# Pre-norm image blocks in four mixers: gate rows of the mLSTM cut into units, its second pass begun inside the first, and the norm of the neighbourhood layer one step ahead

## The chip, the cores and the metric

The kernel runs on one core of a Trainium2 chip, in 32-bit floats. The metric is device time in microseconds (us), the median of three runs. The engines are TensorE (PE), VectorE (DVE), ScalarE (ACT), GpSimd (POOL) and SyncE (SP). Each takes its instructions strictly in order, so an instruction that waits holds all behind it. Each also has a queue from which transfers (DMAs) are issued; here SP and ACT issue them.

## The reference

The input is a batch of 8 images of 32 x 32 tokens with 256 channels. Four layers follow, each `x = x + layer(groupnorm(x))`: retention, mLSTM, neighbourhood attention (7 x 7) and attention on a disc. The change touches the second and the third. The mLSTM, for each image with 1024 tokens, 8 heads and 512 inner channels, is cut to:

```python
up = xs @ W_up.T;  x_m, z = up[..., :512], up[..., 512:]
x_act = silu(conv_b + causal_conv4(x_m))
q, k, v = blockwise 4x4 projections of x_act, x_act, x_m
ig, fg = [q, k, v] @ W_i.T + b_i, [q, k, v] @ W_f.T + b_f
lc = cumsum(log_sigmoid(fg))
logD = where(causal, lc[i] - lc[j] + ig[j], -inf);  m = max_j logD
C = (q k^T / sqrt(64)) * exp(logD - m)
h = (C / (max(|sum_j C|, exp(-m)) + eps)) v
out = ((layernorm(h) * norm_w + skip * x_act) * silu(z)) @ W_down.T
```

The neighbourhood layer adds a learned bias for each head and relative position to the scores of a token with its 49 neighbours and takes a softmax over them.

## The kernel before

Each layer is a function (`layer0` to `layer3`). Activations are kept with channels on the 128 partitions. Between the layers they lie in DRAM, one image as a tile of 128 x 2 x 1024. A ring of three such tiles (`Base.big`, L170) holds images and the large weights in turn: a new tile of the ring waits until the tile three back has been read for the last time.

**mLSTM, `layer1` (L734).** The order of PE and ACT is the order of the program. The order of DVE, POOL and SP is set by a planner from its own costs, so an instruction may stand earlier or later on these than it does in the program. The work runs over 16 segments, each half an image (512 tokens), in two passes.

The first pass is a loop over units `u`, a quarter of a segment each: `project` (PE L808, ACT copy xm L823), `convolve` (ACT L830, three DVE instructions L835), `silu_a` two units later (ACT L841), `silu_z` (L848). In each segment `gates(s-1)` (PE L859, DVE copy L865, four stores from SP L869) makes the gate values of the segment before. Beside it run the group norm of the next image (DVE L194, PE L203, DVE L211, PE L222, POOL L226 and L239) and its load.

The gates of four images make 32 rows of 1024 tokens, one for each head of each image. `rows_sum` (L882) fetches them (SP L892), takes the logarithm of the sigmoid (ACT L895 to L898, DVE), a running sum (DVE L899), a running maximum (L903), stores the maximum and makes three differences (L910 among them). `rows_exp` (L913) takes the exponentials (ACT L917), stores two of them, and turns two row tiles so that tokens lie on partitions (PE L926, DVE L929). For the first four images they are called after `u` = 40 and 46; for the last four in the second pass, before the chunks 1 and 3.

The second pass is a loop over 64 chunks of 128 tokens, four a segment. `load(s)` fetches the activations xa (SP L983), rows of exponentials (low and rb, L993) and xm (xv, L999); `maxima(n)` fetches a 128 x 1024 tile d (L1010), from which POOL makes the masked difference (L1013) and ACT eight exponentials (L1022). In a chunk PE takes `scores` (L1080), whose product with d is DVE's L1086; `queries` of the next chunk (PE L1035, ACT copy g L1037, DVE gr L1040); `keys` (PE L1048, DVE L1052); `value` (PE L1062, ACT copy L1066); then `within` (L1099, L1105), which needs d, `across` (L1119, L1125), which needs gr, and `update` (L1150, POOL L1165, DVE L1169). `units` puts output work of the segment before between them: one part in the chunks t = 0, 1 and 3 of four, none in t = 2; t = 3 has `down` (L1205). PSUM results of one bank's size share a ring of four buffers. `follow(k)` prepares the next layer's first image, k chunks before the end: load at k = 7, statistics (L194) at 5, later the norm and weights.

**Neighbourhood layer, `layer2` (L1619).** It works in 16 steps an image. Here PE, ACT, DVE and POOL are all in program order. Its first instructions are loads from the ACT queue: parameters (L1636), a mask table `win` (L1638), the bias for eight heads (L1641) and the projection's weights (L1643). The bias used is `win - bias` on POOL (L1774), as scores are kept with the opposite sign; the mask table excludes tokens that are no neighbours. Then PE projects (L1667) and ACT or DVE copies with a bias (L1673, L1681, L1683). In a step n the order is: scores of n+1 (PE L1407, DVE L1416), the exponentials of n (ACT L1428) and their division (POOL L1433, `e`), then the `Fillers` units that are due (a unit with due step `at` is emitted in the first step n for which `at <= n`), then the transposes of n-1 (L1447) and the values of n-2 (L1466). Projections of image b start at step 16b - 8; the two halves of its norm (`normed`, POOL L239) are due at 16b - 9 and 16b - 8.5.

Of the kernel before, what the change touches and what calls it, by code (L numbers as in the profile page):

```python
# [16 lines left out]
P = 128  # L17
# [15 lines left out]
def shape_constants():  # L33
# [44 lines left out]
    idx = near_index()  # L78
    k["k_win2"] = np.where(idx >= 0, 0.0, -MASK_OUT).astype(f)


# [28 lines left out]
def layouts(inputs):  # L110
# [29 lines left out]
    a["l2_rpb"] = np.where(idx[:, None] >= 0, rpb[:, idx].transpose(1, 0, 2), 0.0).astype(  # L140
# [593 lines left out]
def layer1(tc, K, src, dst, n_img, a, first):  # L734
# [3 lines left out]
    with tc.tile_pool(name="l1c", bufs=1, reuse_waits="tile") as cp, tc.tile_pool(  # L738
        name="l1w", bufs=1, reuse_waits="tile"
    ) as wk, tc.tile_pool(  # L740
# [11 lines left out]
        def load_x(b):  # L752
            x[b] = K.big("x")
            nc.scalar.dma_start(x[b], src[:, :, b * L : (b + 1) * L])
# [127 lines left out]
        def rows_sum(i):  # L882
            def temps(tag):
                t = wk.tile([P, 2, L], F32, tag=tag, name="row", bufs=2)
                return t[0:NR, 0], t[0:NR, 1]

            (av, f), (sp, lc) = temps("num"), temps("sq")
            cm = wk.tile([NR, 1 + L], F32, name="cm")
            row[i] = av, f, sp, lc, cm
            for g, t in enumerate((av, f)):  # L890
                for b in range(GRP):
                    nc.sync.dma_start(t[8 * b : 8 * b + 8], gated[i][b, g])  # L892
            nc.vector.memset(cm[:, 0:1], MASK_OUT)
            nc.scalar.preload_act_table_set("natural_log_exp_and_others")
            nc.scalar.activation(sp, f, AF.Abs, bias=gbias[0:NR, 1:2])  # L895
            nc.vector.tensor_scalar(f, f, gbias[0:NR, 1:2], 0.0, ALU.add, ALU.min)
            nc.scalar.activation(sp, sp, AF.Exp, scale=-1.0)
            nc.scalar.activation(sp, sp, AF.Ln, bias=epsn[0:NR, 1:2])  # L898
            nc.vector.tensor_tensor_scan(lc, f, sp, 0.0, ALU.add, ALU.subtract)  # L899
            nc.vector.scalar_tensor_tensor(  # L900
                av, av, gbias[0:NR, 0:1], lc, ALU.add, ALU.subtract
            )
            nc.vector.tensor_tensor_scan(cm[:, 1:], av, av, cm[:, 0:1], ALU.max, ALU.max)  # L903
            nc.sync.dma_start(rowd[i][0], cm[:, 1:])


            ends = by_chunk(cm[:, 1:])[:, :, P - 1 : P].to_broadcast([NR, 2 * NCH, P])
            starts = by_chunk(cm[:, 0:L])[:, :, 0:1].to_broadcast([NR, 2 * NCH, P])
            nc.vector.tensor_sub(by_chunk(sp), starts, by_chunk(cm[:, 1:]))
            nc.vector.tensor_sub(by_chunk(f), by_chunk(av), ends)  # L910
            nc.vector.scalar_tensor_tensor(lc, lc, -1.0, cm[:, 1:], ALU.mult, ALU.subtract)

        def rows_exp(i):  # L913
            av, w, r, low, _ = row.pop(i)
            nc.scalar.preload_act_table_set("natural_log_exp_and_others")
            for t in (r, w, low):
                nc.scalar.activation(t, t, AF.Exp)  # L917
            nc.sync.dma_start(rowd[i][1], r)
            nc.sync.dma_start(rowd[i][2], low)

            ps = ring("col_ps")[:, 0 : 2 * 2 * NCH * NR].rearrange(
                "p (i t n) -> p i t n", i=2, n=NR
            )
            for j, t in enumerate((av, w)):
                for k in range(2 * NCH):
                    nc.tensor.transpose(  # L926
                        ps[:, j, k], t[:, k * P : (k + 1) * P], K.ident[0:NR, 0:NR]
                    )
# [1284 lines left out]
```

## Time and profile before

| | us |
|---|---|
| median of three runs | 3490.29 (3487.11 to 3499.76) |
| the profiled execution | 3481.33 |
| its span, first to last instruction | 3479.5 |
| PE busy | 3255.0 |
| ACT busy | 2237.1 |
| DVE busy | 2172.7 |
| POOL busy | 1491.2 |
| mean granted PE clock | 0.964 |
| layer 0 ends, mLSTM's first pass starts | about 1088 |
| second pass starts | about 1373 |
| layer 2 starts | about 2039 |

The clock is a share of full speed. A group in the page names line, engine, operation, output and inputs, shape and count, then busy time and mean, then the idle time of the engine ahead of it with what ended that. A line of the timeline gives start, duration, engine, line, operation, shape and the number of instructions drawn together; in brackets stands the idle time ahead of it and the instruction that ended it.

### The profile page before, as it was taken

The numbers are of one execution on the slowest core, as the hardware profiler recorded it, in microseconds if no ns is written. First come the engines' busy times: TensorE is split into PE (matmuls) and PEld (weight loads), VectorE is DVE, ScalarE is ACT, GpSimd is POOL, SyncE is SP. The second block draws the span as 40 slices with busy tenths as digits, with TensorE's granted clock in tenths as the row PEclk, the third lists the DMA queues.
The fourth block names the chain that finished last, engine by engine and source line by source line (L and its number), as shares of the span: only waits on it lengthen the run. The fifth ranks groups of instructions, "written<-read, shape, count | busy, mean of one in ns | idle before, by whom it ended". The sixth has DMA issues, their size and how long they took to land.

```text
span 3479.5 us, 77392 instructions
## 1 busy us (share of the span) xinstructions
PE 3255.0 (94%) x30760; PEld 1655.6 (48%) x30760; DVE 2172.7 (62%) x5559; ACT 2237.1 (64%) x5022; POOL 1491.2 (43%) x1071
## 2 busy tenths in 40 slices
PE   7999999999998988899999989999998889999998
PEld 3323323323323444677676645555553545555454
DVE  4777677677675664555555545556564667677775
ACT  3667667667675554555555446666675778888885
POOL 4233233232221110345444443333335567777777
PEclk9999999999999998899999999999998889999999
DMA  3000000000003667577777531111111001101001
GB/s 135 13 25 1 25 25 1 25 25 1 25 25 116 236 199 256 162 199 179 203 210 187 136 112 38 38 38 50 50 48 43 2 14 38 32 29 35 26 26 59
DMA packets 139054, 268.44 MB, mean 77 GB/s; under 512 B 9218, under 2 KB 77188, under 8 KB 130372
## 3 DMA queue, kind: packets, MB, share of 16 engines
q1 hardware_dynamic: 131152, 241.90, 23.1%
q10 hardware_dynamic: 7540, 21.60, 1.9%
q8 instruction: 242, 3.96, 0.5%
q14 instruction: 120, 0.98, 0.1%
HBM read 178.27 MB, written 85.20 MB: 76 GB/s over the span
## 4 chain that ended last, share of the span: by engine, by line
PE 68%; ACT 10%; DVE 8%; DMA 5%; POOL 4%; issue 4%; SPq 0%; POOLq 0%; ACTq 0%; DVEq 0%
PE s L633 7%; PE sm L651 6%; PE num L678 5%; PE qkv_ps L1667 5%; PE qkv_ps L1902 4%; PE up_ps L808 3%; PE dn_ps L1205 3%; PE qk_ps L508 3%; DMA x<-x 3%; PE pt L1575 2%; PE pt L1447 2%; PE fac_ps L2004 2%; PE o_ps L561 2%; ACT e L1963 2%; DMA d<-l1rows 2%
## 5 line engine op out<-in xcount | busy, mean ns | idle before, releaser
L639 DVE TENSOR_TENSOR e<-s,ret 128x1024 f32<-128x1024 f32 x512 | 603.0, 1219 | 180.3 <-PE s L633 175.1
L643 ACT ACTIVATE ea<-e 128x1024 f32<-128x1024 f32 x512 | 535.9, 1056 | 267.0 <-DVE e L639 233.4
L633 PE MATMUL s<-qk,qk 32*128 32x512 f32 x2048 | 300.2, 640 | 2.6 <-POOL qk L525 1.9
L1580 DVE COPY pts<-pt 112x512 f32<-112x512 f32 x256 | 176.5, 690 | 181.0 <-PE pt L1575 179.1
L1433 POOL TENSOR_TENSOR e<-e,su 128x616 f32<-128x616 f32 (+2 forms) x128 | 157.4, 1230 | 287.0 <-DVE su L1432 278.8
L1013 POOL TENSOR_TENSOR d<-cmask,d 128x1024 f32<-128x1024 f32 x64 | 152.7, 2386 | 296.0 <-DMA d<-l1rows 183.5
L651 PE MATMUL sm<-ea,ones 128*32 128x512 f32 x2048 | 273.0, 604 | 2.0 <-DVE dn L659 2.0
L678 PE MATMUL num<-e,v 128*32 128x512 f32 x2048 | 266.6, 592 | 0.0
L808 PE MATMUL up_ps<-x,wup 128*128 128x512 f32 x512 | 233.5, 608 | 11.3 <-DVE gate L865 9.3
L1963 ACT ACTIVATE e<-win,disc 128x196 f32<-128x196 f32 x512 | 240.9, 548 | 0.2
L1565 POOL TENSOR_TENSOR e<-e,su 128x784 f32<-128x784 f32 x128 | 191.5, 1496 | 92.3 <-DVE su L1564 67.4
L1557 ACT ACTIVATE e<-e,mx 128x196 f32<-128x196 f32 x512 | 229.1, 456 | 0.0
L1970 POOL TENSOR_TENSOR e<-e,win 128x784 f32<-128x784 f32 x128 | 201.3, 1573 | 38.1 <-issue 32.9
L1667 PE MATMUL qkv_ps<-x,w 128*128 128x512 f32 x384 | 194.7, 644 | 21.3 <-POOL x L239 17.5
L1428 ACT ACTIVATE e<-e,mx 128x154 f32<-128x154 f32 (+2 forms) x512 | 213.4, 429 | 0.2 <-DVE mx L1416 0.2
L1902 PE MATMUL qkv_ps<-xq,w 128*128 128x512 f32 x384 | 199.5, 646 | 11.0 <-DVE kp L1914 5.4
L1575 PEld LDWEIGHTS pt<-idg,e 128*112 128x112 f32 x1024 | 121.1, 141 | 136.9 <-issue 60.1
L1575 PE MATMUL pt<-idg,e 128*112 128x128 f32 x1024 | 167.3, 290 | 19.2 <-DVE pts L1580 8.8
L633 PEld LDWEIGHTS s<-qk,qk 32*128 32x128 f32 x2048 | 85.1, 182 | 184.2 <-issue 121.5
L835 DVE SCALAR_TENSOR_TENSOR cv<-xm,par,cv 128x512 f32<-128x512 f32 x192 | 140.2, 750 | 48.8 <-ACT cv L830 46.2
L1022 ACT ACTIVATE d<-d,cols 128x128 f32<-128x128 f32 x512 | 164.1, 395 | 0.0
L1547 DVE CUSTOM_DVE_ANT_0 e<-s,e 128x196 f32<-128x196 f32 x512 | 154.0, 358 | 12.9 <-PE s L1534 7.8
(241 smaller groups left out, 6644.1 us busy)
## 6 DMA issues: line engine op xcount, KB each, us to landing
d<-l1rows SPq DMA_DIRECT2D x64, 512.0 KB
x<-x SPq DMA_DIRECT2D x25, 1024.0 KB
x<-x SPq DMA_DIRECT2D x32, 512.0 KB
l1xm<-xm SPq DMA_DIRECT2D x16, 1024.0 KB
l1sz<-sz SPq DMA_DIRECT2D x16, 1024.0 KB
xv<-l1xm SPq DMA_DIRECT2D x32, 512.0 KB
l1xa<-xa SPq DMA_DIRECT2D x16, 1024.0 KB
sz<-l1sz SPq DMA_DIRECT2D x16, 1024.0 KB
```

What stands on the lines that cost most here:

```text
L633: nc.tensor.matmul(s[:, j % 2], qk[b, 1, c][g, kb * P : (kb + 1) * P], qk[b, 0, c][g, h * HALF : (h + 1) * HALF], start=True, stop=True,)
L639: nc.vector.tensor_mul(e[n, i], s, m)
L643: nc.scalar.activation(ea[n, i], e[n, i], AF.Abs)
L651: nc.tensor.matmul(acc["sm"][g, :], ones, ea[n, j // 2][:, j % 2, :], start=kb == 0, stop=kb == 7,)
L678: nc.tensor.matmul(acc["num"][g, :], v[b][:, kb, vc], e[n, j // 2][:, j % 2, :], start=kb == 0, stop=kb == 7,)
L808: nc.tensor.matmul(ps, wup[:, kc, m * P : (m + 1) * P], seg(s)[:, kc], start=kc == 0, stop=kc == 1,)
L1428: self.nc.scalar.activation(p[:, j], p[:, j], AF.Exp, scale=-1.0, bias=mx[:, j : j + 1], accum_out=su[:, j : j + 1],)
L1557: self.nc.scalar.activation(e[:, j], e[:, j], AF.Exp, scale=-1.0, bias=mx[:, j : j + 1], accum_out=self.su[:, j : j + 1],)
L1575: self.nc.tensor.transpose(ps[: self.PART, at : at + P], self.tile(n)[:, 2 * i + j, k * self.PART : (k + 1) * self.PART], self.K.ident,)
L1667: nc.tensor.matmul(ps, w[:, kc, o : o + P], x[b][:, kc, h * HALF : (h + 1) * HALF], start=kc == 0, stop=kc == 1,)
L1902: nc.tensor.matmul(ps, w[:, kc, o : o + P], xq[b][:, kc, h * HALF : (h + 1) * HALF], start=kc == 0, stop=kc == 1,)
L1963: nc.scalar.activation(e[:, j], win[:, 0], AF.Tanh, scale=disc[b][:, i, 8 + h : 9 + h], bias=disc[b][:, i, h : h + 1],)
```

## The change

- mLSTM: the memory of the working tiles is laid out ahead of the constants', and the second image has a tile of its own instead of one of the ring.
- `rows(i)` replaces `rows_sum` and `rows_exp`: eleven units with the same instructions. For the first four images one is called in each `u` from 36 to 46. For the last four they follow the chunks 0, 1, 2, 2, 3, 3, 4, 4, 5, 6 and 7, in tiles of the ring.
- `start()`, at `u` = 58 of 67, issues the second pass's first load, three d tiles and two masked differences; queries, keys and values of chunk 0 are taken at `u` = 66, ahead of the last `gates`. The load of rb is a function of its own, `load_rb`, so that segment 0's stays behind the last gates.
- In the second pass the image for the residual is loaded at the first chunk of its image, four chunks later than before. `value(n+1)` follows `within(n)`. The next layer's image is loaded at k = 12 for k = 7.
- Layer 2: the bias table holds the mask value itself, the table `win` is gone, and only the sign is turned, for heads 0 and 1 on ACT, for the others on POOL. `normed` is due half a step earlier, which puts its second half in step 16b - 9 with the first.

The diff, cut; `load`, `load_z`, `maxima`, `masked`, `decays`, `queries`, `keys` and `value` move up unchanged, but for `load`, which loses the rb part and the image:

```diff
@@ -137,7 +133,7 @@
     a["l2_par"] = np.concatenate([_cols(qkv_b), _cols(i["L2_conv_proj_b"])], 1)
     idx = near_index()
     rpb = i["L2_conv_rpb"].reshape(HEADS, -1)
-    a["l2_rpb"] = np.where(idx[:, None] >= 0, rpb[:, idx].transpose(1, 0, 2), 0.0).astype(
+    a["l2_rpb"] = np.where(idx[:, None] >= 0, rpb[:, idx].transpose(1, 0, 2), MASK_OUT).astype(
         rpb.dtype
     )
     a["l3_qkv"] = _wt(i["L3_conv_w_qkv"])
@@ -735,9 +731,9 @@
     nc = tc.nc
     NS = 2 * n_img
     GRP = min(4, n_img)
-    with tc.tile_pool(name="l1c", bufs=1, reuse_waits="tile") as cp, tc.tile_pool(
-        name="l1w", bufs=1, reuse_waits="tile"
-    ) as wk, tc.tile_pool(
+    with tc.tile_pool(name="l1w", bufs=1, reuse_waits="tile") as wk, tc.tile_pool(
+        name="l1c", bufs=1, reuse_waits="tile"
+    ) as cp, tc.tile_pool(
         name="l1p", bufs=1, space=PSUM, reuse_waits="tile"
     ) as pp, tc.manual_schedule(
         engines={mybir.EngineType.PE, mybir.EngineType.Activation}
@@ -749,8 +745,8 @@
         K.ring = ring
         x, xm, xa, sz, conv = ({} for _ in range(5))
 
-        def load_x(b):
-            x[b] = K.big("x")
+        def load_x(b, own=False):
+            x[b] = wk.tile([P, 2, L], F32, name="x1") if own else K.big("x")
             nc.scalar.dma_start(x[b], src[:, :, b * L : (b + 1) * L])
 
         def seg(s):
@@ -879,58 +875,211 @@
         def by_chunk(t):
             return t.rearrange("p (t n) -> p t n", n=P)
 
-        def rows_sum(i):
...
+        def rows(i, temp):
+            q = {}
+            def fetch():
+                for k in ("av", "f"), ("sp", "lc"):
+                    t = temp()
+                    q[k[0]], q[k[1]] = t[0:NR, 0], t[0:NR, 1]
+                q["cm"] = wk.tile([NR, 1 + L], F32, name="cm")
+                for g, k in enumerate(("av", "f")):
+                    for b in range(GRP):
+                        nc.sync.dma_start(q[k][8 * b : 8 * b + 8], gated[i][b, g])
+                nc.vector.memset(q["cm"][:, 0:1], MASK_OUT)
+            def soft():
+                f = q["f"]
+                nc.scalar.activation(q["sp"], f, AF.Abs, bias=gbias[0:NR, 1:2])
+                nc.vector.tensor_scalar(f, f, gbias[0:NR, 1:2], 0.0, ALU.add, ALU.min)
+            def soft2():
+                sp = q["sp"]
+                nc.scalar.preload_act_table_set("natural_log_exp_and_others")
+                nc.scalar.activation(sp, sp, AF.Exp, scale=-1.0)
+                nc.scalar.activation(sp, sp, AF.Ln, bias=epsn[0:NR, 1:2])
+            def sums():
+                nc.vector.tensor_tensor_scan(
+                    q["lc"], q["f"], q["sp"], 0.0, ALU.add, ALU.subtract
+                )
+            def a():
+                nc.vector.scalar_tensor_tensor(
+                    q["av"], q["av"], gbias[0:NR, 0:1], q["lc"], ALU.add, ALU.subtract
+                )
+            def most():
+                av, cm = q["av"], q["cm"]
+                nc.vector.tensor_tensor_scan(cm[:, 1:], av, av, cm[:, 0:1], ALU.max, ALU.max)
+                nc.sync.dma_start(rowd[i][0], cm[:, 1:])
+            def before():
+                cm = q["cm"]
+                starts = by_chunk(cm[:, 0:L])[:, :, 0:1].to_broadcast([NR, 2 * NCH, P])
+                nc.vector.tensor_sub(by_chunk(q["sp"]), starts, by_chunk(cm[:, 1:]))
+            def within():
+                ends = by_chunk(q["cm"][:, 1:])[:, :, P - 1 : P]
+                nc.vector.tensor_sub(
+                    by_chunk(q["f"]), by_chunk(q["av"]), ends.to_broadcast([NR, 2 * NCH, P])
+                )
+            def low():
+                nc.vector.scalar_tensor_tensor(
+                    q["lc"], q["lc"], -1.0, q["cm"][:, 1:], ALU.mult, ALU.subtract
+                )
+            def exps():
+                nc.scalar.preload_act_table_set("natural_log_exp_and_others")
+                for k in ("sp", "f", "lc"):
+                    nc.scalar.activation(q[k], q[k], AF.Exp)
+                nc.sync.dma_start(rowd[i][1], q["sp"])
+                nc.sync.dma_start(rowd[i][2], q["lc"])
+            def turned():
+                ps = ring("col_ps")[:, 0 : 2 * 2 * NCH * NR].rearrange(
+                    "p (i t n) -> p i t n", i=2, n=NR
+                )
+                for j, k in enumerate(("av", "f")):
+                    for t in range(2 * NCH):
+                        nc.tensor.transpose(
+                            ps[:, j, t], q[k][:, t * P : (t + 1) * P], K.ident[0:NR, 0:NR]
+                        )
+                nc.vector.tensor_copy(cols[i], ps)
+            return [fetch, soft, soft2, sums, a, most, before, within, low, exps, turned]
...
+        def load_rb(s):
+            b, h = divmod(s, 2)
+            rows, r8 = rowd[b // GRP], 8 * (b % GRP)
+            rb[s] = wk.tile([P, 4, 3 + HALF], F32, tag="xm", name="rb", bufs=2)
+            for p in range(2):
+                r = rows[1][r8 + p : r8 + p + 1, h * HALF : (h + 1) * HALF]
+                nc.sync.dma_start(
+                    rb[s][64 * p : 64 * p + 64, :, 0:HALF],
+                    bass.AP(r.tensor, r.offset, [[0, 64], [2 * L, 4], [1, HALF]]),
+                )
...
+        def start():
+            load_x(0)
+            load(0)
+            for n in range(3):
+                maxima(n)
+            masked(0)
+            masked(1)
         with tc.tile_pool(name="l1g", bufs=1, space=PSUM, reuse_waits="tile") as gp:
             if n_img > 1:
-                load_x(1)
+                load_x(1, True)
+            units = {}
+            for i in range(NG - 1):
+                todo = rows(i, lambda: wk.tile([P, 2, L], F32, tag="num", name="row", bufs=2))
+                for k, f in enumerate(todo):
+                    units.setdefault(8 * GRP * (i + 1) + 4 + k, []).append(f)
             for u in range(4 * NS + 3):
                 s, c = divmod(u, 4)
                 if s < NS:
@@ -949,124 +1098,28 @@
                     silu_a(*divmod(u - 2, 4))
                 if u < 4 * NS:
                     silu_z(s, c)
+                if NG > 1 and u == 4 * NS - 6:
+                    start()
+                if NG > 1 and u == 4 * NS + 2:
+                    queries(0)
+                    keys(0)
+                    value(0)
                 if c == 2 and s:
                     gates(s - 1)
-                i, k = divmod(u - 8 * GRP, 8 * GRP)
-                if 0 <= i < NG - 1 and k == 8:
-                    rows_sum(i)
-                if 0 <= i < NG - 1 and k == 14:
-                    rows_exp(i)
+                for f in units.get(u, []):
+                    f()
         nc.scalar.preload_act_table_set("natural_log_exp_and_others")
+        late = rows(NG - 1, lambda: K.big("row"))
         if NG == 1:
-            rows_sum(0)
-            rows_exp(0)
...
+            for f in late:
+                f()
+            start()
+            queries(0)
+            keys(0)
+            value(0)
+            late = []
+        at = (0, 1, 2, 2, 3, 3, 4, 4, 5, 6, 7)
+        late = {n: [f for m, f in zip(at, late) if m == n] for n in range(2 * NCH)}
...
@@ -1227,7 +1280,7 @@
             def follow(k):
 
                 nx = K.next
-                if k == 7:
+                if k == 12:
                     nx.load()
                 if k == 5:
                     for i in range(4):
@@ -1243,26 +1296,18 @@
 
             def prefetch(n):
                 s, t = divmod(n, NCH)
+                if n and n % (2 * NCH) == 0:
+                    load_x(s // 2)
                 if t == 0 and s + 1 < NS:
                     load(s + 1)
+                    load_rb(s + 1)
                 if t == 3 and s < NS:
                     load_z(s)
 
-            load(0)
-            for n in range(3):
-                maxima(n)
-            masked(0)
-            masked(1)
-            queries(0)
-            keys(0)
-            value(0)
+            load_rb(0)
             decays(0, range(4))
             for n in range(N):
                 prefetch(n)
-                if NG > 1 and n == 1:
-                    rows_sum(NG - 1)
-                if NG > 1 and n == 3:
-                    rows_exp(NG - 1)
                 if n + 3 < N:
                     maxima(n + 3)
                 if n + 2 < N:
@@ -1274,14 +1319,16 @@
                 if n + 1 < N:
                     decays(n + 1, (0, 1))
                     keys(n + 1)
-                    value(n + 1)
                 units(n, 1)
                 within(n)
                 if n + 1 < N:
+                    value(n + 1)
                     decays(n + 1, (2, 3))
                 units(n, 2)
                 across(n)
                 update(n)
+                for f in late.get(n, []):
+                    f()
                 if K.next:
                     follow(N - n)
             for n in range(N, N + NCH):
@@ -1634,8 +1681,6 @@
         x[0], w = first.x, first.w
         par = cp.tile([P, 8], F32, name="par2")
         nc.scalar.dma_start(par, a["l2_par"])
-        win = cp.tile([P, nbias], F32, name="win2")
-        nc.scalar.dma_start(win, a["k_win2"])
         bias = cp.tile([P, HEADS, nbias], F32, name="bias2")
         for h in range(HEADS):
             nc.scalar.dma_start(bias[:, h], a["l2_rpb"][:, h])
@@ -1697,6 +1742,12 @@
                     t[:, 704:].rearrange("p (s i j) -> p s i j", s=2, j=14), cols(5, 8, 14)
                 )
 
+        def negated(h):
+            if h < 2:
+                nc.scalar.activation(bias[:, h], bias[:, h], AF.Copy, scale=-1.0)
+            else:
+                nc.gpsimd.tensor_scalar(bias[:, h], bias[:, h], -1.0, None, ALU.mult)
         cur, strips = {}, {}
         vunits = [[t for t in pairs if len(t.parts) == 1]]
         vunits += [[t] for t in pairs if len(t.parts) == 2]
@@ -1738,7 +1789,7 @@
                 fill.add(16 * b - 11, lambda: gn.mean(b))
                 fill.add(16 * b - 10, lambda: gn.root(b))
                 for c in range(2):
-                    fill.add(16 * b - 9 + c / 2, lambda c=c: normed(b, c))
+                    fill.add(16 * b - 9.5 + c / 2, lambda c=c: normed(b, c))
             units = []
             for c in range(2):
                 for s in (2, 0, 1):
@@ -1770,8 +1821,7 @@
                 for c in range(2):
                     fill.add(n - 6 + c, lambda c=c: nx.norm(c))
             for h in range(HEADS):
-                at = -8.4 if h < 4 else h - 4
-                fill.add(at, lambda h=h: nc.gpsimd.tensor_sub(bias[:, h], win, bias[:, h]))
+                fill.add(-4.5 if h < 4 else h - 4, lambda h=h: negated(h))
             fill.emit(-1)
 
             def front(n):
```

## The prediction

> **What bounds the kernel now.** I read the page first (busy shares, slices, costliest groups), then busy time and granted clock in windows, then the timeline of each stretch where the clock dips. The page says TensorE:
>
> ```profile
> PE 3255.0 (94%) x30760; PEld 1655.6 (48%) x30760; DVE 2172.7 (62%) x5559; ACT 2237.1 (64%) x5022; POOL 1491.2 (43%) x1071
> ...
> L1667 PE MATMUL qkv_ps<-x,w 128*128 128x512 f32 x384 | 194.7, 644 | 21.3 <-POOL x L239 17.5
> ```
>
> No matmul is removed, so only time in which TensorE idles, or runs slowly, can go. In the mLSTM's second pass it is 98% busy at clock 1.00; the dips lie where stages meet and where gate rows are made. In the window rows the columns are stretch, length, busy us of PE, weight loads, DVE, ACT, POOL, then clock, DMA share, GB/s; PE is busy 34.91 of 50 us and slow besides:
>
> ```profile
> 1400.00:1450.00 50.00, 34.91 (x443) 29.41 (x442) 30.03 (x40) 27.12 (x58) 12.47 (x7) 0.80 0.49 152
> 1500.00:1550.00 50.00, 48.12 (x543) 33.75 (x540) 25.06 (x49) 24.06 (x62) 23.82 (x16) 1.00 0.87 205
> ```
>
> **The change part by part.** Each term is a delay of the PE chain, the path that sets the end.
>
> *1. Layer 0 to 1.* Constants get memory free earlier, and the second image a tile of its own. Before, ScalarE's first copy waits 13.06 us for a constant, and TensorE idles 2.46 us at L203 (first line of the next fence). Convolutions catch up slowly behind the copy, so I take 2; bounds 0 and the 7.4 us that PE idles between 1068 and 1090, most of which belongs to layer 0's tail.
>
> *2. First half's gate rows.* Two lumps (L882, L913) become eleven units in eleven steps of 5 us; their count and their queues stay. Before:
>
> ```profile
> 1110.02 0.35 PE L203 MATMUL gn_ps<-gn_mv,idg 128*128 128x2 f32 x2 [2.46 <-ACT cv L830]
> ...
> 1279.91 3.45 PE L808 MATMUL up_ps<-x,wup 128*128 128x512 f32 x4 [7.92 <-DVE gate L865]
> ```
>
> The second says that DVE's gate copy (L865) stood behind the lump. L203 runs once an image: at 1142.66, 1175.25, 1207.87, 1240.89, then 1283.19 and 1326.70, so 32.6 us an image and then 42.3 and 43.5: 20.6 lost. The transposes at L926 remain (two stretches of 0.68). The row operations are 10.2 us of DVE in all, and the planner still gathers them within two or three units, between convolutions. Their cover is TensorE's supply of finished copies, and DVE otherwise waits 7 us an image for x at L194. If the cover is gone, a unit waits up to the scan's 2.3 us, and the gate copy is late next. ScalarE's three exponentials (1.0 each, with a table load of 1.28) now stand in one unit before the copies of xm that PE's projection needs. POOL's masked tile of chunk 0 is now ahead of its part of a copy. So 1 to 7 us of stalls stay: gain 14, bounds 8 and 19.
>
> *3. Second pass begun within the first, and second half's rows.* Before:
>
> ```profile
> 1373.20 4.41 SPq L869 DMA_DIRECT2D l1gates<-gate  x4
> 1377.71 0.50 SPq L983 DMA_DIRECT2D xa<-l1xa  x1
> 1378.32 4.92 SPq L993 DMA_DIRECT2D rb<-l1rows  x2
> 1386.33 13.68 SPq L892 DMA_DIRECT2D row<-l1gates  x8
> 1400.12 2.30 SPq L1010 DMA_DIRECT2D d<-l1rows  x2
> ...
> 1385.92 2.04 PE L1035 MATMUL g_ps<-xa,bdg 128*128 128x128 f32 x8 [13.11 <-DMA xa<-l1xa]
> 1415.54 0.43 PE L1099 MATMUL sums<-d,hot 128*32 128x128 f32 x8 [4.72 <-DVE d L1086]
> 1421.68 0.66 PE L1099 MATMUL sums<-d,hot 128*32 128x128 f32 x8 [5.72 <-DVE d L1086]
> ```
>
> PE waits 13.11 for the activations, which SP issues behind four gate stores; in chunks 2 and 3 the product d stands behind the lump on DVE. Chunk 0's scores ran at 1390.46, chunk 4's at 1440.73, its L1099 at 1445.12. After: activations, values and d tiles are issued some 40 us earlier, and queries, keys and values of chunk 0 run before the last gates, so chunk 0's scores come at about 1375. Chunks without output units took 6.4 us (1390.46 to 1396.81): chunk 1 at 1381.5. Its gr needs rb, which SP still issues behind the last gate stores (1377.7 plus 4.92); by xa's 8.2 us from issue to use it lands near 1386, and holds L1119 of chunk 1 by some 1 to 3 us. Then SP issues xa and rb of segment 1 (0.5 and 4.9) and eight row fetches (13.68): done near 1402. ScalarE's first row operation waits in order for them, ahead of the copy g of chunk 3 (0.6), so scores of chunk 3 come near 1404. The d load of chunk 4 is issued behind the fetches at 1402, takes 10 to 12 us, then 2.4 on POOL (L1013), 1.3 on ScalarE, 1.3 on DVE: its L1099 near 1418 against 1445.12. Gain 27; bounds 18 (both loads late by a further queue's worth, 9) and 38 (all stalls gone: 51 us from 1390 to 1441 less 26, plus 13).
>
> Here the Trainium skill has a rule against it: "GPSIMD Engine Reference", Specifications, says that GpSimd's memory interfaces are shared with VectorE and contend with DVE instructions of two memory inputs. The trace agrees: L903 took 2.33 us alone and 4.32 beside POOL's L1013, L910 1.21 and 3.35. Row work beside masked tiles is thus 10.2 plus 4.9, about 15 us. As one lump it would cost PE those 5 us; as units of at most 4.3, a chunk having 9.4 us and DVE 56% busy (313.7 of 560), it is covered. I take 0.
>
> *4. Load of the next layer's image five chunks earlier* (k=12 for 7). The store before it in its lane and L194's statistics decide:
>
> ```profile
> 1915.59 1.29 DVE L194 BATCH_NORM_STATS2 gn_st<-x 128x6 f32<-128x512 f32 x2 [8.45 <-DMA x<-x]
> ...
> 1918.72 2.08 PE L1062 MATMUL vt_ps<-bdv,xv 128*128 128x128 f32 x8 [8.89 <-DVE gr L1040]
> ```
>
> The statistics block DVE, and PE waits behind gr. Its segment takes 51.9 us (1890.06 to 1941.8) for 37.5. The load now lacks the wait on the store, but the planner pulls the statistics forward too, so part stays: gain 9, bounds 4 and 13. The weight loads behind it on SP move with it.
>
> *5. Layer 2's start.* The mask table's load goes; the bias loads wait for VectorE and GpSimd, no longer for the last projection.
>
> ```profile
> 2039.63 8.89 ACTq L1641 DMA_DIRECT2D bias<-l_rpb  x8
> 2050.60 1.27 ACT L1673 ACTIVATE qT<-qkv_ps,par 128x512 f32<-128x512 f32 x2 [25.84 <-DMA xr<-x]
> 2051.34 3.43 PE L1667 MATMUL qkv_ps<-x,w 128*128 128x512 f32 x4 [3.77 <-ACT qT L1673]
> ```
>
> qT stands behind these issues; they can now start when POOL's last product ends (2034), so qT comes before PE needs it. PE gets back 3.77 and the slowness of 3.43 for 1.8, less two new sign flips on ScalarE ahead of the value copies (about 1 us each by its 128x1024 rows at 1.06): gain 5, bounds 0 and 9. The other six flips are one-input work on POOL in place of a two-input subtraction of 2.09 us: no dearer, off the path.
>
> *6. Norm a step ahead.* One step is 4.49 us. Before, the second half of each image's norm (L239) runs at 2161.70, behind e at 2160.72, and L1667 waits:
>
> ```profile
> 2162.94 4.54 PE L1667 MATMUL qkv_ps<-x,w 128*128 128x512 f32 x6 [2.51 <-POOL x L239]
> ```
>
> and the window just behind that gap, with the granted clock 0.51 in the third column from the end:
>
> ```profile
> 2164.00:2167.00 3.00, 3.00 (x5) 1.17 (x4) 0.75 (x1) 0.00 (x0) 0.00 (x0) 0.51 0.90 280
> ```
>
> Eight take 8.0 us (2159.31 to 2167.32), unstalled 3.55: 4.46 for each of six images, 2.4 for another. After, it follows the first half at 2159.07 and ends at 2160.3, before PE asks. "TensorE: Matmul & The Clock Gate" (HAM oscillation) says that gaps over about 3.4 us cost clock: by it a gap of 2.51 costs only itself, 17.5 in all (the page's group above). The row shows 0.51 in the 3 us behind the gap and 4.54 for six matmuls instead of 2.7. The trace decides: 6 x 4.46 + 2.4 = 29; I take 27 for remainders on POOL, bounds 17 and 30. e at 2160.72 is not delayed.
>
> *7. Values behind the within step.* Eight matmuls (1.06 us) that covered the time from scores to d leave that place. Where output units fill it (three chunks of four), DVE is done anyway. In the fourth, DVE's L1086 ends 2.5 us after scores begin (1648.22 to 1651.89) less what queries and keys cover, some 0.9: 16 x 0.9 = 14 lost. Against it, waits of vt and dn on DVE's gr go (8.9 of vt is term 4; vt 2.2 and dn 3.1 stay), and values not demanded early free a buffer in the ring: about 0.6 a segment. Taken at 0, bounds -14 and +8.
>
> Sum: 2 + 14 + 27 + 9 + 5 + 27 + 0 = 84 off the span 3479.5, so 3395.5; the profiled execution, 3481.3, becomes 3397, and the median 3490.3 (the profiled one is 9 under it) 3406.
>
> **Rivals.** *A: the stalls return in another form.* The planner still bunches row work, ScalarE waits in order for the row fetches, POOL's masked tiles block copies, DMAs are full around 1386 (share 1.08). Terms 2 to 4 give 8 + 18 + 4 in place of 50: 64 less, 3426; with the other lower bounds too, 3450. *B: values later cost their 14*, all else right: 3420. *C, slower: PE waits for d in every chunk.* Place: L1099 in all 64; the price is a further wait per chunk, and 84/64 = 1.3 us is where it decides; at 2 us, 128 - 84 = 44 slower, 3534. Against: before, 48 of 64 chunks have output work there. *D: the norm's step doesn't move the wait* since POOL puts e first: 27 less, 3433; the order of POOL's instructions speaks against it.
>
> **How the numbers follow.** Sum 0.60, A 0.18, B 0.10, D 0.05, C 0.05, no effect 0.02. Range 3382 to 3446: below by 24, the upper bounds of terms 2 to 4 partly together; above, A, B and D. About 0.5% (17 us) is what a measurement of this kernel can tell from no change. Faster 0.93, same 0.02, slower 0.05.
>
> **What would show it.** L203 stays near 33 to 36 us apart throughout; no 13 us gap before L1035; chunk 4's L1099 some 27 us sooner behind the last gates; the segment of the image load under 43; no POOL x wait at qkv and its clock 1.00; a segment of the second pass at 37.5. It is wrong if that segment grows, or if the largest waits reappear with DVE or ScalarE as releaser.

## The result: 0.6% faster, a quarter of the forecast

The changed kernel takes 3470.72 us (median; 3467.34 to 3474.51) against 3493.23 for the kernel before on the same chip: a ratio of 0.9936, 95% interval 0.9913 to 0.9958. That is some 22 us; the forecast was 84, and 3470.7 lies above its range. The profiled execution's span fell from 3479.5 to 3467.1, by 12.4. Three stages gave what was forecast and two gave less. The second pass, which was to gain 9 us, lost 43, and the last layer's end, whose code is unchanged, took 7 longer.

The page after, its line of engines and the group of the neighbourhood layer's projection, whose wait on POOL was 17.5:

```profile
span 3467.1 us, 77413 instructions
PE 3269.6 (94%) x30760; PEld 1658.0 (48%) x30760; DVE 2168.6 (63%) x5559; ACT 2231.6 (64%) x5024; POOL 1489.6 (43%) x1069
...
L1712 PE MATMUL qkv_ps<-x,w 128*128 128x512 f32 x384 | 181.3, 609 | 1.3 <-POOL x L235 1.3
```

The wait is gone. To see where the time went, I read the same PE instruction in both timelines at each border of a stage:

| stage, by PE's timeline | before | after | gain | forecast |
|---|---|---|---|---|
| second norm of the first pass (L203, now L199) at | 1142.66 | 1140.84 | 1.8 | 2 (step 1) |
| from there to the last norm of the first pass | 184.0 | 175.8 | 8.2 | 14 (step 2) |
| from there to scores of chunk 8 | 151.5 | 131.4 | 20.1 | 27 (step 3) |
| from there to scores of chunk 63 | 531.5 | 575.0 | -43.5 | 9 (steps 4, 7) |
| from there to layer 2's first scores | 49.2 | 43.7 | 5.5 | 5 (step 5) |
| from there to its last image's first output | 512.3 | 484.7 | 27.6 | 27 (step 6) |
| from there to the end | 908.3 | 915.7 | -7.4 | 0 |

In the second pass these are PE's largest waits between 1450 and 2015, in a list that names the engine, what waited and for whom, then us in all, times and the longest. Before:

```profile
PE vt_ps L1062 <- DVE gr L1040: 11.1, 8, 8.9
PE dn_ps L1205 <- DVE gr L1040: 3.1, 5, 0.6
```

and after:

```profile
PE sums L1152 <- DVE d L1139: 41.4, 15, 14.3
```

A new wait stands where `within` (L1152) needs the product d: 15 times, 13 of them in the chunk t = 2, which has no output work, once in every segment from the third on but one. The longest, 14.3, is in that one segment, in its chunk t = 1: there the product stands on DVE behind statistics that wait 14.48 us for the next layer's image. One of the others, in the timeline after (PE, DVE and POOL in turn):

```profile
1629.10 1.16 PE L1133 MATMUL sc<-g,xa 64*128 64x128 f32 x16
...
1636.50 1.16 PE L1152 MATMUL sums<-d,hot 128*32 128x128 f32 x16 [4.72 <-DVE d L1139]
1634.40 0.41 DVE L1222 TENSOR_TENSOR state<-decayed,kv_ps 64x256 f32<-64x256 f32 x1 [4.32 <-POOL decayed L1218]
...
1635.67 1.28 DVE L1139 TENSOR_TENSOR d<-d,sc 128x512 f32<-128x512 f32 x2
1631.00 2.34 POOL L1008 TENSOR_TENSOR d<-cmask,d 128x1024 f32<-128x1024 f32 x1 [14.56 <-DMA d<-l1rows]
1633.30 1.06 POOL L1218 TENSOR_TENSOR decayed<-state,rb 128x520 f32<-128x520 f32 x1
```

Read backwards: PE waits for the product of this chunk (L1139); that stands in DVE's queue behind the state of the chunk before (L1222), which waits for POOL's `decayed` (L1218), which stands behind the masked difference of the *next* chunk (L1008), and that waits 14.56 us for its transfer. So a d tile that is not due for another chunk holds PE now. The length of POOL's wait is not new: for the same tile it was 14.15 us in the kernel before. What is new is its end: there POOL began the masked difference 6.2 us ahead of the scores of the chunk in which PE waits here (1642.00 and 1648.22), now it begins 1.9 us behind them.

### The profile page after: what moved, and what is told of

The parts are those of the page before. It is cut to its first block, busy times and chain, and to the rows that moved or that the text cites. A ratio compares the mean times of both kernels' runs of the same rounds, so it can differ in the third digit from the quotient of the medians.

```text
span 3467.1 us, 77413 instructions
## 1 busy us (share of the span) xinstructions
PE 3269.6 (94%) x30760; PEld 1658.0 (48%) x30760; DVE 2168.6 (63%) x5559; ACT 2231.6 (64%) x5024; POOL 1489.6 (43%) x1069
## 4 chain that ended last, share of the span: by engine, by line
PE 70%; ACT 9%; DVE 7%; DMA 6%; POOL 4%; issue 4%; POOLq 0%; SPq 0%; ACTq 0%; DVEq 0%
PE s L629 7%; PE sm L647 6%; PE num L674 5%; PE qkv_ps L1712 5%; PE qkv_ps L1952 4%; PE up_ps L804 3%; PE dn_ps L1258 3%; PE qk_ps L504 3%; PE pt L1622 3%; DMA d<-l1rows 3%; PE pt L1494 2%; DMA x<-x 2%; PE fac_ps L2054 2%; PE o_ps L557 2%; PE num_ps L1158 2%
## 5 line engine op out<-in xcount | busy, mean ns | idle before, releaser
L1008 POOL TENSOR_TENSOR d<-cmask,d 128x1024 f32<-128x1024 f32 x64 | 151.9, 2375 | 375.7 <-DMA d<-l1rows 218.3
L1712 PE MATMUL qkv_ps<-x,w 128*128 128x512 f32 x384 | 181.3, 609 | 1.3 <-POOL x L235 1.3
L1061 ACT COPY vt<-vt_ps 128x512 f32<-128x512 f32 x64 | 37.4, 584 | 221.5 <-PE vt_ps L1057 221.5
```

What stands on the lines that cost most here:

```text
L1712: nc.tensor.matmul(ps, w[:, kc, o : o + P], x[b][:, kc, h * HALF : (h + 1) * HALF], start=kc == 0, stop=kc == 1,)
```

## What the runs showed

Each time below is the median of the run, and each ratio is to the kernel before on the same chip, with its 95% interval. "The stretch" is the time from scores of chunk 8 to scores of chunk 48 in the run's profile: 380 us before, 412 after.

**Which part costs.** First the suspects one by one, on the changed kernel.

```diff
                     keys(n + 1)
+                    value(n + 1)
                 units(n, 1)
                 within(n)
                 if n + 1 < N:
-                    value(n + 1)
                     decays(n + 1, (2, 3))
```

> The changed kernel with one part undone: values stand again between keys and the first output units. In the changed kernel the stretch from scores of chunk 8 to scores of chunk 48 took 412 us, before 380. If the later values are the main cause (either as lost cover on TensorE or because the planner then issues the load of sz ahead of a d tile), the stretch falls to 385 to 392 us and the time from 3471 to 3445 to 3452. If the new place of the image load is the main cause, it falls by less than 10 us, to 402 or more, and the time stays above 3460.

3419.4 us, 0.9797 (0.978 to 0.9813); the stretch 379.7. This one part undone gives 51 us (49 by the ratios), more than expected, and the whole pace of before. The other suspect, the image's place:

```diff
-                if n and n % (2 * NCH) == 0:
-                    load_x(s // 2)
+                if n == 2 * NCH:
+                    load_x(1)
+                if n > 2 * NCH and n % (2 * NCH) == NCH and n + NCH < N:
+                    load_x(s // 2 + 1)
```

> The changed kernel with the residual's image loaded four chunks earlier again, for images 2 to 7; values stay late. If the new place of this load (beside the low rows, the store and two d tiles of an even segment) is the main cause, even segments fall from 44 to about 40.5 us, the stretch of chunks 8 to 48 from 412 to about 394, and the time to about 3450. If the later values are, the waits only move to the odd segments: the stretch stays over 405 and the time within 6 us of 3471.

3459.4, 0.9917 (0.9902 to 0.9932); the stretch 416.9. The time is 11 us lower, from what lies ahead of chunk 8 (4 us in the profile) and behind chunk 48 (10), but the stretch is 5 longer: the long chunks t = 2 only moved to odd segments (14 to 16 us in three of them), as the second of the two expectations had it. Both together:

> Values put back and images loaded four chunks earlier. If these two account for the second pass, chunks 8 to 48 take 380 us again as before, and the time is 3471 less 32, about 3438. If something else in the change slows the steady pass, 5 us or more stay above 380.

3425.7, 0.982 (0.9806 to 0.9835); the stretch 379.9. Nothing is left for the image's place to explain in the stretch, and with values put back the earlier load makes the median 6 us higher. And the part alone, in the kernel before (the reverse of the first diff, there):

> The kernel before with one part of the change alone: values behind the within step. If the late values cost by themselves what putting them back gave (44 to 51 us), this is 35 to 50 us slower than before: 3525 to 3540. If they cost that only beside the image load's new place, less than 20: under 3510. The prediction's bound for this part was 14 slower.

3548.8, 1.0168 (1.0144 to 1.0191): 58 us slower, more than either expectation. The part costs 51 us in the changed kernel and 58 in the one before.

**By which way it costs.** Lost cover on PE was the prediction's way. The transfers are another. SP's queue in the segment before the wait shown above, after the change:

```profile
1592.23 0.34 SPq L974 DMA_DIRECT2D xa<-l1xa  x1
1602.35 0.34 SPq L998 DMA_DIRECT2D sz<-l1sz  x1
1602.79 0.37 SPq L1005 DMA_DIRECT2D d<-l1rows  x1
1603.26 1.25 SPq L983 DMA_DIRECT2D xv<-l1xm  x2
1604.61 2.61 SPq L991 DMA_DIRECT2D rb<-l1rows  x2
1609.48 0.83 SPq L1264 DMA_DIRECT2D x<-x  x1
1610.41 1.46 SPq L1005 DMA_DIRECT2D d<-l1rows  x1
1613.28 8.58 SPq L977 DMA_DIRECT2D low<-l1rows  x4
1622.47 5.68 SPq L1005 DMA_DIRECT2D d<-l1rows  x2
```

and with values put back, the same segment:

```profile
1581.29 0.34 SPq L974 DMA_DIRECT2D xa<-l1xa  x1
1582.79 0.34 SPq L983 DMA_DIRECT2D xv<-l1xm  x1
1585.32 0.37 SPq L1005 DMA_DIRECT2D d<-l1rows  x1
1585.74 1.82 SPq L983 DMA_DIRECT2D xv<-l1xm  x1
1591.77 1.39 SPq L991 DMA_DIRECT2D rb<-l1rows  x2
1593.21 0.92 SPq L998 DMA_DIRECT2D sz<-l1sz  x1
1598.23 0.55 SPq L1264 DMA_DIRECT2D x<-x  x1
1599.15 0.43 SPq L1005 DMA_DIRECT2D d<-l1rows  x1
1600.79 3.44 SPq L977 DMA_DIRECT2D low<-l1rows  x4
1606.28 8.28 SPq L1005 DMA_DIRECT2D d<-l1rows  x2
```

The last value of a segment, taken in its chunk t = 2, frees a buffer of xv. When it comes later, the loads of xv come later, and the planner, which orders SP by when it believes a buffer free, puts the load of sz ahead of d, xv and rb. SP then stands for 10 us (1592.6 to 1602.4) behind xa, until POOL has released the buffer of sz; then six transfers (sz, d, two of xv, two of rb) go out within 5 us. Counted from the segment's first scores, xv goes out 10 us later than with values put back; the value itself ends only 4 later (at 1597.3), so the larger part of that delay is SP's standing. SP's waits for that buffer between 1450 and 1860 (us in all, times, longest), after and with values put back:

```profile
SPq L998 <- POOL num L1253: 102.3, 10, 13.0
SPq L998 <- POOL num L1253: 21.8, 5, 5.9
```

The d tile that PE waits for in the chunk shown above is the one issued at 1610.41, behind this bunch. It does not go out later in its segment than with values put back (2.3 us ahead of the segment's first scores, there 1.1), but it takes 20.6 us from its issue until POOL begins on it; there, from 1599.15, it takes 14.2, and POOL begins 3.8 us ahead of the scores of that chunk:

```profile
1613.35 2.35 POOL L1008 TENSOR_TENSOR d<-cmask,d 128x1024 f32<-128x1024 f32 x1 [15.56 <-DMA d<-l1rows]
```

The order on SP alone was tried first, with an edge that keeps sz behind rb while values stay late:

```diff
-                nc.sync.dma_start(
+                last_rb[s] = nc.sync.dma_start(
...
-            nc.sync.dma_start(sz[s], szd[s])
+            i = nc.sync.dma_start(sz[s], szd[s])
+            if s + 1 in last_rb:
+                tc.add_manual_dep(
+                    getattr(i, "ins", i), getattr(last_rb[s + 1], "ins", last_rb[s + 1]).name,
+                    mybir.DependencyInfo(
+                        mybir.DependencyClass.NoSync, mybir.DependencyReason.DATA
+                    ),
+                    reason="order",
+                )
```

> The changed kernel with values late, and one ordering edge: on SP the load of sz stands behind the two loads of rb of its segment, as it mostly did before, no longer ahead of a d tile. If it is SP's order that makes d late, this does as much as putting values back: chunks 8 to 48 in 385 to 395 us, time 3445 to 3455. If it is the lost cover on TensorE, nothing comes back: 405 to 412 us, time within 6 us of 3471.

3478.1, 0.9968 (0.9956 to 0.998); the stretch 420.7. Inconclusive: with sz behind, a load of rb went to the front in every other segment and SP stood for 11 us at that instead. Then the transfer was left out:

```diff
-                if t == 3 and s < NS:
+                if t == 3 and s < 2:
                     load_z(s)
+                elif t == 3:
+                    sz[s] = sz[s - 2]
```

> The changed kernel, values late, with the loads of sz left out from the third segment on (the tiles of the first two segments are used again, so the outputs of the later segments are wrong). It frees SP of a wait and the queues of 1 MB a segment. If a part of the cost of the late values is d arriving late behind bunched transfers, the waits for d of 2 to 5 us in the chunks without output work shrink to the 1 us that missing cover explains: chunks 8 to 48 from 412 to about 392 to 398 us, the time to 3450 or less. If all of it is lost cover on TensorE, the stretch stays above 405 and the time within 6 us of 3471.

3457.0, 0.99 (0.9875 to 0.9926); the stretch 406.6. This decides nothing either: the time is 14 us lower, but the stretch stays above 405, and in every other segment SP stands for rb again (10.9 us from 1592.4 to 1603.3). The run that separates the two ways moves no value at all; it only keeps xv back about as long as late values do (`order_after` adds such an edge to the last matmul of the within step, here as a wait; it stands on the kernel with values put back):

```diff
-                nc.sync.dma_start(xv[s, i], xmd[s][:, 2 * i : 2 * i + 2])
+                j = nc.sync.dma_start(xv[s, i], xmd[s][:, 2 * i : 2 * i + 2])
+                if s >= 2:
+                    order_after(tc, j, K.within[NCH * (s - 1) - 2], True)
```

> Values put back everywhere on TensorE, but the loads of xv are held until the within step of the chunk t = 2, as late values held them; on SP the order of the loads is then again that of the changed kernel. If the loss is transfers that bunch behind the held xv (d late), the waits come back without any value moved: 20 to 45 us slower than 3419, so 3440 to 3465, chunks 8 to 48 over 395. If it is TensorE's lost cover alone, the time stays within 5 us of 3419 and the stretch at 380 to 383.

3452.2, 0.9894 (0.9871 to 0.9918); the stretch 399.6. In the stretch SP issues its 151 loads in the order of the changed kernel, one for one, it stands 107.5 us for the buffer of sz, and the same d tile takes 18.3 us from issue to POOL. With PE's order untouched, 33 of the 51 us are lost again, so the larger part of the loss is transfers. How much of it is the later xv and how much the order that comes with it was not separated. Which chunk it enters by (in the chunk t = 2 `value(n + 1)` follows `keys(n + 1)` again):

```diff
                     keys(n + 1)
+                    if n % NCH == 2:
+                        value(n + 1)
...
                 if n + 1 < N:
-                    value(n + 1)
+                    if not (n % NCH == 2):
+                        value(n + 1)
```

> The changed kernel, in which values stay late in the chunks that have output work (three of four), and stand early again in the chunk without (t = 2). If all of the loss comes from the chunk without output work, this is as fast as values put back everywhere (3419) or up to 8 faster; chunks 8 to 48 in 375 to 382 us. If the loss is spread over all chunks, it lies near 3458, a quarter of the way.

3432.2, 0.9837 (0.982 to 0.9854); the stretch 389.8. The reverse of it:

> The reverse: values late in the chunk t = 2 only, early in the other three. If the chunk t = 2 carries the loss, the time is that of the changed kernel, 3465 to 3480, and chunks 8 to 48 take 405 to 415 us. If it is spread, about 3432.

3454.7, 0.9901 (0.988 to 0.9923); the stretch 397.9. Against 3419.4, late in t = 2 costs 35 us and late in the other three 13; 48 of 51; each run lies between what was expected if one chunk carried the loss and if it were spread. By which way the three cost their 13 was not tried. In the last run SP's order is again that of the changed kernel, and 35 is near the 33 of the held xv. The bare loss of cover can be seen in its odd segments, where no wait for a transfer comes on top: t = 2 takes 8.2 us where it took 6.9. That is 1.3 a segment, where the prediction had 0.9; in 16 segments it would be 21 us. Cover and transfers need not add up: where PE waits for a transfer, the missing cover lies within that wait.

**The smaller shortfalls.** In the first pass of the changed kernel one wait of PE over 1.1 us is left, in PE's, ACT's and POOL's timelines:

```profile
1280.14 0.56 PE L199 MATMUL gn_ps<-gn_mv,idg 128*128 128x2 f32 x2 [6.42 <-ACT cv L826]
1277.07 0.78 ACT L826 ACTIVATE cv<-xm,par 128x512 f32<-128x512 f32 x1 [6.11 <-POOL xm L816]
1274.55 2.34 POOL L1008 TENSOR_TENSOR d<-cmask,d 128x1024 f32<-128x1024 f32 x1 [25.56 <-DMA d<-l1rows]
1276.84 0.20 POOL L816 COPY xm<-xm 128x12 f32<-128x12 f32 x1
```

POOL stands 25.56 us at the first masked difference, which is wanted some 90 us later, and the 0.2 us copy of xm's edge stands behind it, ahead of ACT's convolution. On the kernel with values put back, the first four were held behind the last such copy:

```diff
-            masked(0)
-            masked(1)
...
                 if NG > 1 and u == 4 * NS + 2:
+                    for n in range(2):
+                        order_after(tc, masked(n), K.copied)
                     queries(0)
...
```

> The changed kernel with values put back, and the first four masked differences kept behind the last copy of xm's edge on POOL. The single wait of 6.4 us at the group norm's matmul in the first pass, in which POOL's copy stands behind the first masked difference, should go: 7 to 9 us faster than the kernel with values put back alone (3419), so 3410 to 3413. If the wait has another cause, or the differences now delay chunk 0, no more than 3 us come.

3419.7, 0.9795 (0.9773 to 0.9817). That wait (6.6 us with values put back) is gone, one of 2.2 on DVE takes its place, and the last norm stands at 1313.0 instead of 1317.0; but by chunk 48 the kernel is only 0.6 us ahead, and the median doesn't move. The statistics that wait for the next layer's image, held behind gr of chunk 58:

```diff
-                if k == 5:
+                if k == 7:
+                    K.tc, K.edge = tc, K.gr
                     for i in range(4):
                         nx.stats(i)
+                    K.edge = None
...
             j = nc.vector.bn_stats(self.st[:, c, h, :], parts[c][h])
+            if getattr(self.K, "edge", None):
+                order_after(self.K.tc, j, self.K.edge, True)
```

> The changed kernel with values put back, and the statistics of the next layer's image held on DVE behind gr of chunk 58, instead of where the planner puts them, eight chunks earlier. The wait of 8.9 us at the value matmul (behind gr, behind statistics that wait for the image) should go with the half clock after it: 10 to 14 us faster than the kernel with values put back alone, so 3405 to 3410. If the transfers around it are what is late, the wait moves to d and less than 5 come.

3419.6, 0.9793 (0.9769 to 0.9817). The wait of 8.9 at the value matmul is gone and chunk 63 comes 7.3 us sooner (1971.9 for 1979.2), the first output of layer 2's last image 4.8; the end of this profile comes 2.7 later, and the median doesn't move. And the earlier load of that image, undone (`k == 7`):

> Values put back, and the next layer's image loaded at k = 7 again. The prediction gave 9 us to the earlier load. If that was right, this is 7 to 11 slower than 3419. If the statistics, which the planner moves with the load, keep the wait, it is within 4 us of 3419 and the wait of about 9 us at the value matmul only stands one segment later.

3423.6, 0.981 (0.9794 to 0.9827): 4 us slower than values put back alone, not the 7 to 11 that the prediction's gain would be, and the intervals of the two overlap. PE's waits for it, first with the load at 12, then at 7:

```profile
1846.79 2.05 PE L1057 MATMUL vt_ps<-bdv,xv 128*128 128x128 f32 x8 [8.92 <-DVE gr L1035]
```

```profile
1919.98 2.05 PE L1057 MATMUL vt_ps<-bdv,xv 128*128 128x128 f32 x8 [8.37 <-DVE gr L1035]
```

The wait only stands elsewhere, with the statistics that the planner moves along. Then three repairs together: the masked differences and the statistics held back as above, and values early, first in t = 2 alone:

> Three repairs together on the changed kernel: values early in the chunk t = 2 only, the first four masked differences behind the last copy on POOL, and the next image's statistics behind gr of chunk 58. Each of the last two gave 4 to 7 us in its stage, of which the median of its own run showed nothing; together with the first 3400 to 3415 if they add up, 3419 if the stages behind give it back.

3421.9, 0.981 (0.979 to 0.983): 10 us under values early in t = 2 alone (3432.2). The same with values early everywhere:

> Values put back everywhere, the first four masked differences behind the last copy on POOL, the next image's statistics behind gr of chunk 58. The two repairs shortened their stages by 4 and 7 us in the profiles, but not the medians of their own runs. If the stages add, 3408 to 3413; if what they give is taken back behind them (in the second pass by the transfers, in the last layer by its granted clock), 3417 to 3422.

3416.5, 0.979 (0.9774 to 0.9806): the fastest of all, 2.1% under the kernel before and 1.5% under the changed one, though no more than 3 us under putting values back alone.

**The norm alone**, half a step earlier in the kernel before (`16 * b - 9.5` for `16 * b - 9`):

> The kernel before, with the norm of the neighbourhood layer half a step earlier and nothing else. The prediction gave this 27 us, with the half clock behind the gap, and 17.5 by the rule that such a gap costs only itself. By the row: 3490 less 25 to 29, so 3461 to 3465, and 67.3 us an image in place of 71.8. By the rule: 3471 to 3474, and 69.3 an image.

3463.2, 0.9923 (0.9903 to 0.9944): 25 us less than the kernel before of its session, and 67.3 us from one image's first output to the next's. In the windows of its trace at this place PE is busy throughout and the clock (third from the end) is full:

```profile
2161.00:2164.00 3.00, 3.00 (x8) 1.32 (x7) 0.91 (x9) 1.25 (x5) 1.53 (x2) 1.00 0.74 277
2164.00:2167.00 3.00, 3.00 (x56) 1.80 (x55) 1.62 (x10) 2.58 (x10) 0.00 (x0) 1.00 0.02 5
```

## Why the prediction was wrong

- **Step 7, values behind the within step, is the one that failed.** It was taken at 0, with -14 as its worst; the runs give -51 (part undone) and -58 (part alone). It counted PE's missing cover in the chunk t = 2 (0.9 a segment forecast, 1.3 seen) and the waits of vt and dn that would go, and did. It did not ask what the moved instruction *releases*. The last value of a segment frees the buffers of xv; moved behind `within`, it moves SP's loads of 1 MB, and the planner's order with them. Holding xv alone costs 33 us. The step treated the move as one on PE's queue and looked at no other queue. It also put the other three chunks at nothing, as output units would fill the place; they cost 13. With this part alone undone, the rest of the change gives 3419.4, inside the forecast range.
- Rival A came true in its terms: steps 2, 3 and 4 gave 8, 20 and at most 4 us where it put 8, 18 and 4. It alone would have been 3426, still in the range. Rival B had the right part and sign, and the wrong way; its 14 us were a quarter of the cost. Rival C had the right wait (PE for d) and the wrong chunks: it came in one chunk of four, at up to 4.8 us and once 14.3, not in all.
- **Step 4 also failed.** It gave 9 us to the earlier load, with 4 as the least; with values put back the wait kept its size (8.92 for 8.89) in another segment, and the medians give the earlier load no more than 4. That the planner pulls the statistics forward with the load stood in the step; it takes the whole wait along, not a part. In the changed kernel it holds up d instead of gr, for 14.3.
- Step 2 gave 8.2 for 14, at its lower bound. The largest stall that stayed is one that it named, POOL's masked tile ahead of the copy: 6.4 us.
- Step 3 gave 20.1 to chunk 8 for 27. Chunk 4's L1099 (now L1152) came at 1405.07, sooner than the forecast 1418. What failed is the cover of row work on DVE, taken at 0 whole: the product d of chunk 4 stands between row instructions, and PE waits 1.41 and 2.42 us for its halves. Behind these waits the matmuls take almost twice their time (1.98 us below; 1.09 in other chunks), and the granted clock is 0.50 from 1408 to 1414:

```profile
1405.07 0.43 PE L1152 MATMUL sums<-d,hot 128*32 128x128 f32 x8 [1.41 <-DVE d L1139]
1407.91 0.65 PE L1152 MATMUL sums<-d,hot 128*32 128x128 f32 x8 [2.42 <-DVE d L1139]
1408.50 1.98 PE L1158 MATMUL num_ps<-d,vt 128*64 128x128 f32 x16
```

  So chunk 4 takes 16.5 us to the next scores where the kernel before took 7.8. In this place a unit, not the sum, is what PE sees, and the clock adds to it; step 6 counted the clock behind a gap, step 3 did not.
- The rule on shared memory interfaces (the Trainium skill, "GPSIMD Engine Reference", Specifications), weighed in step 3, hardly mattered here: the second half's row instructions took 11.9 us of DVE after (0.73, 2.96, 1.53, 2.33, 1.94, 1.21, 1.21), nearer to 10.2 alone than to 15. Three of them lay beside a masked tile for a part of their time; the scan that began ahead of one, at 1404.95, took 2.33 as if alone, and the masked tile beside it took 3.34 for some 2.36.
- Step 6 was right, in size and by the reason given: 27.6 in the profile, 25 alone by the medians, against 17.5 if the gap had cost only itself. The row decided against the rule of 3.4 us (the Trainium skill, "TensorE: Matmul & The Clock Gate", HAM oscillation): a gap of 2.51 was followed by a lower clock in all six images that had it (0.51 to 0.61 in the 3 us behind it).
- Steps 1 and 5 were right: 1.8 for 2, 5.5 for 5.
- Two numbers of the prediction don't follow from its own terms: with all other lower bounds too, rival A is 3457, not 3450; and the 2.5 us of step 7 run from the end of the scores, not from their beginning, from which it is 3.67.
- The end, unchanged code, lost 7.4 us in this profile, for which no step had a term; the last section returns to it.

## What to carry to other kernels

When an instruction moves, write down what its end releases (a buffer, and so a load, and so a place in a queue) before what it covers; here the release cost 33 of 51 us. Where a planner orders a queue by when it believes buffers free, look at that queue's order in both kernels, not only at the engine that was changed. And when the reader of a transfer moves forward together with it, the wait moves too and is not removed.

## What was not expected of the hardware

The last layer's code and order were the same in all kernels, yet from layer 2's last image's first output to the end the profiled executions took 908.3 us (before), 915.7 (after), and between 908.9 and 920.2 in the others. Where it took longer the granted clock was lower: 0.88 and 0.96 in its last two stretches of 425 us before, 0.87 and 0.95 after; 0.86 and 0.95 where it took 920.2. Its length doesn't follow when the layer starts (919.4 with the start at 2540, 908.3 at 2571, 914.2 at 2632). What sets it was not tried. It is as large as some repairs here: one that brought the first output of layer 2's last image 4.8 us forward ended 2.7 us later, so a few microseconds won in an earlier stage can't be read off the total of this kernel.
